# A graph layer: the first batch's source rows counted and multiplied instead of gathered

## The chip, the cores and the metric

The kernel runs on one core of a Trainium2 chip. A core has a matrix engine (PE, with its weight loads shown as PEld), a vector engine (DVE), an activation engine (ACT), GpSimd (POOL) and SyncE (SP, which only issues DMAs here). The metric is the device time of one execution in microseconds (us); the median of the runs is compared. Besides, one execution is recorded by the profiler; its span runs from its first to its last recorded instruction.

## What is computed

One attention layer on a graph of 12,500 nodes with 64 features and 400,000 edges with 64 features, which are sorted by destination. `W_attn` has 192 rows and one column, so an edge's raw score is a number for its source plus one for its destination plus one for its own features. The softmax runs over the edges that end in the same node.

```
h_src = x[src];  h_dst = x[dst]
e = leaky_relu(concat(h_src, h_dst, efeats) @ W_attn + b_attn, 0.01)
m = concat(h_src, efeats) @ W_ne
alpha = softmax of e over the edges of one dst
z = segment_sum(alpha * m, dst)
out = layernorm(x + relu(concat(x, z) @ W_out))
```

`src` is uniform over the nodes. `dst` is floor(12500 u^2) of a uniform u, sorted: the low nodes have many edges (node 0 alone has some 3,600, and the first 8,192 edges end in nodes 0 to 5) and the high ones few.

## The kernel before

**Groups, lots, batches.** The edges are cut into 782 groups of 512: 128 partitions by T = 4 edges in a row. Sixteen groups make a batch (47 of these, then 12, 12 and 6 groups: 50 batches), and SG = 4 groups make a lot, so that a batch has four lots. Since the edges are sorted, a group has its destinations in a narrow window of nodes, `widths[k]` wide (4 nodes in the first batches, 48 at most).

**Source rows.** `gather` (L199 to L210) fetches x[src] for a lot into one buffer `zx` by 16 indirect DMAs on POOL, each for 128 edges. There are ZB = 8 such buffers, two batches' worth, so that batch k's lot i is gathered into the buffer that batch k-2's lot i used, when the matmuls that read it (L428) are through. Rows come from `table` in DRAM: 65 numbers each, the node's score as a source ahead of its 64 features. The table must be built first (L518 to L523), so batch 0 is "plain": it is gathered from `x` itself while the table is built, and its source scores are computed from the rows (L244, L246).

**The front** (L448 to L539) reads x into `xall` (13 DMAs on SP), computes each node's score as a destination (`dots`, L489) and as a source, writes the table, broadcasts each group's first destination to all partitions (`d0b`, L529 and L530), and fetches each group's window of destination scores by seven indirect DMAs on POOL (`window`, L483). The first window stands behind three lots' gathers in POOL's order; batch 0's scores need it.

**A batch** has three stages, in an order written out by hand for PE, DVE, ACT and SP (the loop L705 to L786):
- `scores` (L231) for each lot: edge features (`ze`, loaded by SP at L192, three buffers) times their weights, the source's and the destination's score, sums into `yraw`. It also copies `ze` beside the gathered rows (L238), so that a row of `zx` holds both, and makes `hot`, one-hot over the window of destinations (L249).
- `softmax` (L329): running maxima and sums along the edges by scans, with edge values carried between partitions by small PE transposes (`to_line` L265, `to_col` L268). At four places, where DVE waits for PE, it calls `fill`, which is `meanwhile` (L690): one lot's finished products are added into `acc` (L445), and half a lot of waiting products is issued.
- `weights` (L408), one-hot times softmax, and `products` (L423): for each 128 edges a matmul with `zx` as the stationary side and the weights as the moving one. Stationary rows 1 to 128 are the source's and the edge's features, so a lot's sums for both come out of one matmul. The first NOW = 2 lots' products follow the softmax; the other two go into the fills of the next batch's softmax.

`add_in` adds a lot's PSUM bank into `acc`, a ring of 3072 nodes with 128 rows (source features above, edge features below). When a block of NBC = 4 x 128 nodes can get no more edges (`due`, computed ahead from the expected positions with a safety), `finish0` to `finish3` turn it into output rows, and its piece of the ring is cleared. The first block is due after batch 10.

**Safety.** Positions and widths are written into the code, so columns such as `fars`, `ups`, `lates` and `earlies` collect how far the data strays; `raised` (L557) makes one flag of them, and with the flag up a second kernel path computes the result in another way.

The changed places are the constants, `listed`, `edges`, `scores`, `products`, `add_in`, the front's order and the loop.

Of the kernel before, what the change touches and what calls it, by code (L numbers as in the profile page):

```python
# [9 lines left out]
F32 = mybir.dt.float32  # L10
I32 = mybir.dt.int32
# [19 lines left out]
EW = 65  # L31
ZB = 8
HB = 5
RING = 3072
NBC = 4
LATE = 8.0
NOW = 2

BF16 = mybir.dt.bfloat16
# [3 lines left out]
def sorted_path(ctx, tc, x, dst, idx, edge, w_ne, w_attn, b_attn, w_out, out, flag):  # L43
# [41 lines left out]
    widths = [width(b0 + G) for b0, G in zip(starts, sizes)]  # L85

    eps_col = const.tile([P, 1], F32, name="eps_col")
    nc.vector.memset(eps_col, EPS)
# [23 lines left out]
    d0i = const.tile([1, NG], I32, name="d0i")  # L112
    lates = const.tile([P, len(sizes)], F32, name="lates")
    d0b = const.tile([P, NG], F32, name="d0b")
    fars = const.tile([P, len(sizes)], F32, name="fars")
    ups = const.tile([P, len(sizes)], F32, name="ups")
    earlies = const.tile([P, len(sizes)], F32, name="earlies")
    both = const.tile([P, D], F32, name="both")
# [32 lines left out]
    pps = psum.tile([P, 512], F32, name="pps", bufs=1)  # L151
    pp, pens, w_dst = cut(pps, T * BS, 2 * P, D)
    pp = pp.rearrange("p (t g) -> p t g", t=T)
    pens = pens[0:1].rearrange("o (k i) -> o k i", k=2)

    def listed(k):

        g0, G = starts[k], sizes[k]
        srcs = chunks.tile([P, BS, 2 * T], I32, name="srcs", bufs=3)
        last = g0 + G == NG  # L160
        if last:
            nc.vector.memset(srcs, 0)
            nc.sync.dma_start(out=srcs[0:RP, G - 1], in_=idx[NG - 1, P - RP:P])
        for a in range(0, G - last, SG if k == 0 else G):
            b = min(a + (SG if k == 0 else G), G - last)
            nc.sync.dma_start(out=srcs[:, a:b], in_=idx[g0 + a:g0 + b].rearrange("g p c -> p g c"))
        return srcs
# [63 lines left out]
    def scores(g0, n, zx, drel, b0, plain):  # L231

        b = g0 - b0
        r = rows_of(g0, n)
        Sk = widths[starts.index(b0)]
        ze, wrow = fetched.pop(g0)
        nc.scalar.activation(win[0:r, 0:n, 0:Sk], wrow[0:r, 0:n, :], AF.Copy)  # L237
        nc.scalar.activation(zx[0:r, 0:n, :, EW:EW + D], ze[0:r, 0:n], AF.Copy)  # L238
        pr = feats.tile([P, SG, T, D], F32, name="pr", bufs=1)
        nc.vector.tensor_tensor(pr[0:r, 0:n], ze[0:r, 0:n],  # L240
                                w_edge[0:r].unsqueeze(1).to_broadcast([r, n, T, D]), op=OP.mult)
        nc.vector.tensor_reduce(ysum[0:r, 0:n], pr[0:r, 0:n], axis=AX.X, op=OP.add)  # L242
        if plain:
            nc.vector.tensor_tensor(pr[:, 0:n], zx[:, 0:n, :, 1:EW],  # L244
                                    w_src.unsqueeze(1).unsqueeze(1).to_broadcast([P, n, T, D]), op=OP.mult)
            nc.vector.tensor_reduce(zx[:, 0:n, :, 0], pr[:, 0:n], axis=AX.X, op=OP.add)  # L246
        nc.vector.tensor_tensor(ysum[0:r, 0:n], ysum[0:r, 0:n], zx[0:r, 0:n, :, 0], op=OP.add)
# [6 lines left out]
        nc.vector.tensor_tensor(at[0:r, 0:n], hot[0:r, 0:n],  # L254
                                win[0:r, 0:n, 0:Sk].unsqueeze(2).to_broadcast([r, n, T, Sk]), op=OP.mult)
        sdst = tiny.tile([P, SG, T], F32, name="sdst")
        nc.vector.tensor_reduce(sdst[0:r, 0:n], at[0:r, 0:n], axis=AX.X, op=OP.add)  # L257
        nc.vector.tensor_tensor(yraw[0:r, :, b:b + n].rearrange("p t g -> p g t"), ysum[0:r, 0:n], sdst[0:r, 0:n], op=OP.add)
        return hot

# [162 lines left out]
    def products(k, pg, zx, w, groups, r=P):  # L423

        for g in groups:
            for t in range(T):
                if k + 2 < len(sizes):
                    nc.tensor.matmul(pg[:, g, :], zx[:, g, t, 1:EW + D], w[:, g, t, :],  # L428
# [6 lines left out]
    def add_in(g0, n, pg, b0, fac):  # L435
# [4 lines left out]
        for g in range(n):  # L440
            if g == 0 and fac is not None:
                a1 = acc[:, ds(vs[0], 1)]
                nc.vector.tensor_scalar(a1, a1, fac, None, op0=OP.mult)
            ag = acc[:, ds(vs[g], Sk)]
            nc.vector.tensor_tensor(ag, ag, pg[:, g, :], op=OP.add)  # L445

# [8 lines left out]
    nc.scalar.dma_start(out=wout, in_=w_out.rearrange("(h k) o -> k h o", h=2))  # L455
    lists = {0: listed(0)}
    xts = []
# [12 lines left out]
    nc.sync.dma_start(out=d0i, in_=dst.rearrange("(o n) -> o n", o=1)[:, 0:E:GE])  # L470
    lists[1] = listed(1)
    sd = const.tile([P, NB], F32, name="sd")
# [8 lines left out]
    with before:  # L481
# [22 lines left out]
        with tc.manual_schedule(engines={EngineType.DVE, EngineType.Pool, EngineType.Activation, EngineType.PE, EngineType.SP}):  # L504
            lots0 = [(g0, min(SG, sizes[0] - g0)) for g0 in range(0, sizes[0], SG)]
            ahead = [gather(g0, n, lists[0], 0, True) for g0, n in lots0[:-1]]
            for c0 in range(0, NB, CB):
# [24 lines left out]
            for r in range(RING, N, RING):  # L532
                nc.vector.tensor_scalar(turns_, d0f, float(RING), -float(RING), op0=OP.is_ge, op1=OP.mult)
                nc.vector.tensor_tensor(d0i if r + RING >= N else d0f, turns_, d0f, op=OP.add)
            window(0)
            ahead += [gather(g0, n, lists[0], 0, True) for g0, n in lots0[-1:]]
            for k in range(1, NW):
# [8 lines left out]
    nc.tensor.transpose(pwt[0:D, 0, :], wne, ident)  # L546
    wt = work.tile([D, NBC, P], F32, name="xtt", bufs=3)
    nc.vector.tensor_copy(wt[:, 0, :], pwt[0:D, 0, :])
# [29 lines left out]
    def finish1(c0, pxt):  # L578
        n = min(NBC, NB - c0)
        xtt = work.tile([D, NBC, P], F32, name="xtt", bufs=3)  # L580
        nc.scalar.activation(xtt[:, 0:n, :], pxt[0:D, 0:n, :], AF.Copy)
        return c0, xtt
# [65 lines left out]
    for c0 in range(0, NB, NBC):  # L648
# [4 lines left out]
        due[k].append(c0)  # L653
    nc.vector.memset(earlies, 0.0)

    with loop:
# [33 lines left out]
        def meanwhile():  # L690

            add_up(1)
            some_products()

        with tc.manual_schedule(engines={EngineType.PE, EngineType.DVE, EngineType.Activation, EngineType.SP}):
            ready = {}
            for k in range(2):
                as_floats(k, lists[k])
                ready[k] = slots_of(k)
            about = between(0)  # L700
            at_ends(*about)
            nc.scalar.dma_start(out=wins[0], in_=wks[0])
            ahead_of(*flat[0])
            turned_x, ready_x, open_ = finish0(0), None, None
            for k, G in enumerate(sizes):  # L705
# [3 lines left out]
                more = k + 2 < len(sizes)  # L709
                if more:  # L710
# [3 lines left out]
                tiles = [ahead.pop(0) if ahead else gather(g0, n, srcs, b0, k == 0) for g0, n in lots[k]]  # L714
                parts = []
                after = None
                for i, (g0, n) in enumerate(lots[k]):
                    if g0 in follows:
                        ahead_of(*follows[g0])
                    if k == 0 and i == len(lots[k]) - 1:  # L720
# [3 lines left out]
                    hot = scores(g0, n, tiles[i], drel, b0, k == 0)  # L724
                    parts.append((g0, n, tiles[i], hot))
                    if i == 0:
# [14 lines left out]
                    if final and i == 1:  # L741
# [6 lines left out]
                        fronts.append(front(*x1, pps[:, T * BS + 2 * P + D:512].rearrange("p (j d) -> p j d", d=D), False))  # L748
                fac, carry = softmax(k, about, carry, meanwhile)
                while later:  # L750
                    some_products()
# [474 lines left out]
```

## Time and profile before

| what | value |
|---|---|
| median of 3 timed runs | 4614.47 us (4612.89 to 4615.68) |
| the profiled execution's own time | 4585.16 us |
| its span | 4583.4 us |
| granted TensorE clock, mean | 0.995 |
| first gather / first gather of batch 2 / of batch 3 | 4.87 / 194.81 / 286.26 us |
| first gather of batch 47 / last gather | 4341.90 / 4523.8 us |
| DMA traffic | 51 GB/s over the span |

Busy time of each engine in some stretches of the span, in us, with the number of instructions:

| stretch | PE | DVE | ACT | POOL |
|---|---|---|---|---|
| 0 to 97 | 6.14 (16) | 61.69 (106) | 12.06 (34) | 68.62 (78) |
| 97 to 177 | 13.00 (61) | 25.40 (60) | 9.64 (24) | 60.38 (64) |
| 195 to 287 | 29.86 (141) | 24.73 (70) | 10.33 (27) | 60.94 (65) |
| 470 to 562 | 29.70 (141) | 26.50 (75) | 10.56 (28) | 60.50 (65) |

In the profile's lines "L206" is line 206 of the kernel; "zx<-table,srcs" names what an instruction writes and reads; "x64" is a number of instructions. A line of a timeline gives start, duration, engine, line and operation, and in brackets the engine's idle time ahead of it with what ended it; "issue" is waiting that the profile can't name, "remote" a signal from outside the engine. Neighbouring instructions of one kind share a line. An fp32 matmul appears as two records of PE, each with its weight load.

### The profile page before, as it was taken

The numbers are of one execution on the slowest core, as the hardware profiler recorded it, in microseconds if no ns is written. First come the engines' busy times: TensorE is split into PE (matmuls) and PEld (weight loads), VectorE is DVE, ScalarE is ACT, GpSimd is POOL, SyncE is SP. The second block draws the span as 40 slices with busy tenths as digits, with TensorE's granted clock in tenths as the row PEclk, the third lists the DMA queues.
The fourth block names the chain that finished last, engine by engine and source line by source line (L and its number), as shares of the span: only waits on it lengthen the run. The fifth ranks groups of instructions, "written<-read, shape, count | busy, mean of one in ns | idle before, by whom it ended". The sixth has DMA issues, their size and how long they took to land. (4 is left out here: it accounts for less than half of the span.)

```text
span 4583.4 us, 29058 instructions
## 1 busy us (share of the span) xinstructions
PE 1591.8 (35%) x7451; PEld 1535.3 (33%) x7451; DVE 1682.0 (37%) x4079; ACT 629.6 (14%) x1550; POOL 2959.3 (65%) x3142
## 2 busy tenths in 40 slices
PE   0223323232333333333343343333333433343444
PEld 0223323232333333333343333333332433343344
DVE  6223323232333223423343343334333434343445
ACT  1101101011111111111111111111111112111212
POOL 7666666666666666666666666666666666666662
PEclk9999999999999999999999999999999999999998
DMA  8222222122222221222222221222222222222221
GB/s 115 47 44 47 59 44 48 43 59 45 44 55 54 46 45 44 66 45 45 45 67 46 46 56 42 52 54 56 46 59 46 47 46 59 57 46 48 51 46 34
DMA packets 453432, 234.18 MB, mean 51 GB/s; under 512 B 298849, under 2 KB 403272, under 8 KB 453256
## 3 DMA queue, kind: packets, MB, share of 16 engines
q0 software_dynamic: 100320, 104.34, 11.7%
q1 hardware_dynamic: 349892, 127.61, 11.5%
q8 instruction: 60, 0.98, 0.1%
q14 instruction: 116, 0.95, 0.1%
q10 hardware_dynamic: 3044, 0.29, 0.1%
HBM read 225.34 MB, written 6.66 MB: 51 GB/s over the span
## 5 line engine op out<-in xcount | busy, mean ns | idle before, releaser
L206 POOL DMA_INDIRECT zx<-table,srcs x3064 | 2890.7, 943 | 1537.1 <-issue 1301.2
L428 PEld LDWEIGHTS pg<-w,zx 128*128 128x128 f32 x6112 | 1359.4, 329 | 970.9 <-issue 829.8
L428 PE MATMUL pg<-w,zx 128*128 128x12 f32 (+11 forms) x6112 | 1335.8, 376 | 987.8 <-issue 842.0
L240 DVE TENSOR_TENSOR pr<-ze,fixed 128x1024 f32<-128x1024 f32 (+2 forms) x200 | 239.2, 1196 | 511.5 <-ACT fixed L237 325.5
L265 PE MATMUL lines<-ident,bnd 128*1 128x128 f32 x200 | 58.7, 396 | 849.8 <-issue 476.6
L265 PEld LDWEIGHTS lines<-ident,bnd 128*1 128x1 f32 x200 | 9.7, 85 | 861.8 <-issue 500.8
L382 DVE TENSOR_TENSOR_SCAN dens<-rw,lines 1x64 f32<-1x64 f32 (+2 forms) x50 | 13.6, 272 | 637.3 <-remote 517.8
L242 DVE TENSOR_REDUCE fixed<-pr 128x16 f32<-128x1024 f32 (+2 forms) x200 | 240.7, 1204 | 8.9 <-DVE pr L240 2.1
L387 DVE SCALAR_TENSOR_TENSOR soft<-mask,lines,soft 128x128 f32<-128x128 f32 x50 | 18.0, 360 | 597.4 <-remote 512.5
L268 PE MATMUL lines<-ident,line 1*128 1x1 f32 x200 | 36.9, 251 | 534.5 <-issue 279.2
L363 DVE SCALAR_TENSOR_TENSOR soft<-pen,lines,soft 128x128 f32<-128x128 f32 x50 | 18.0, 360 | 549.2 <-remote 457.1
L268 PEld LDWEIGHTS lines<-ident,line 1*128 1x128 f32 x200 | 28.4, 199 | 547.1 <-issue 281.9
L238 ACT ACTIVATE zx<-ze 128x1024 f32<-128x1024 f32 (+2 forms) x200 | 207.9, 1039 | 10.7 <-issue 1.8
L445 DVE TENSOR_TENSOR acc<-acc,pg 128x12 f32 (+11 forms) x782 | 141.0, 180 | 181.7 <-remote 108.6
L268 PE MATMUL lines<-ident,keep 1*128 1x1 f32 x49 | 12.8, 261 | 488.3 <-issue 176.7
L268 PEld LDWEIGHTS lines<-ident,keep 1*128 1x128 f32 x49 | 8.7, 177 | 499.2 <-issue 353.6
L237 ACT ACTIVATE fixed<-wrow 128x144 f32<-128x144 f32 (+10 forms) x200 | 50.6, 253 | 712.4 <-issue 355.5
L257 DVE TENSOR_REDUCE sdst<-pr 128x16 f32<-128x192 f32 (+12 forms) x200 | 116.8, 584 | 27.0 <-DVE pr L254 12.3
L249 DVE TENSOR_TENSOR hot<-fixed,drel 128x576 bf16<-128x576 f32 (+10 forms) x200 | 117.9, 589 | 17.2 <-issue 5.9
L254 DVE TENSOR_TENSOR pr<-hot,fixed 128x576 f32<-128x576 bf16 (+10 forms) x200 | 116.9, 585 | 18.2 <-issue 5.4
L272 ACT ACTIVATE line<-dens 1x256 f32<-1x256 f32 x50 | 32.7, 653 | 657.5 <-DVE dens L384 484.7
L403 ACT ACTIVATE keep<-part,dens 1x1 f32<-1x1 f32 x49 | 14.4, 293 | 708.5 <-DVE part L401 528.1
(153 smaller groups left out, 1497.7 us busy)
## 6 DMA issues: line engine op xcount, KB each, us to landing
ze<-in_edge_dram SPq DMA_DIRECT2D x188, 512.0 KB
zx<-table,srcs POOLq DMA_INDIRECT x3064
table<-xall SPq DMA_DIRECT2D x7, 455.0 KB
out_dram<-yo SPq DMA_DIRECT2D x24, 128.0 KB
ze<-in_edge_dram SPq DMA_DIRECT2D x8, 384.0 KB
edges_of<-in_dst_dram SPq DMA_DIRECT2D x187, 8.1 KB
srcs<-in_idx_dram SPq DMA_DIRECT2D x46, 64.0 KB
xall<-in_x_dram SPq DMA_DIRECT2D x13, 224.0 KB
```

What stands on the lines that cost most here:

```text
L206: nc.gpsimd.indirect_dma_start(out=zx[0:r, g, t, 1:EW] if plain else zx[0:r, g, t, 0:EW], out_offset=None, in_=x[:, :] if plain else table ...
L237: nc.scalar.activation(win[0:r, 0:n, 0:Sk], wrow[0:r, 0:n, :], AF.Copy)
L238: nc.scalar.activation(zx[0:r, 0:n, :, EW:EW + D], ze[0:r, 0:n], AF.Copy)
L240: nc.vector.tensor_tensor(pr[0:r, 0:n], ze[0:r, 0:n], w_edge[0:r].unsqueeze(1).to_broadcast([r, n, T, D]), op=OP.mult)
L242: nc.vector.tensor_reduce(ysum[0:r, 0:n], pr[0:r, 0:n], axis=AX.X, op=OP.add)
L249: nc.vector.tensor_tensor(hot[0:r, 0:n], slots[0:r, 0:Sk].unsqueeze(1).unsqueeze(1).to_broadcast([r, n, T, Sk]), drel[0:r, :, b:b + n].rea ...
L254: nc.vector.tensor_tensor(at[0:r, 0:n], hot[0:r, 0:n], win[0:r, 0:n, 0:Sk].unsqueeze(2).to_broadcast([r, n, T, Sk]), op=OP.mult)
L257: nc.vector.tensor_reduce(sdst[0:r, 0:n], at[0:r, 0:n], axis=AX.X, op=OP.add)
L265: nc.tensor.transpose(in_order(line), col, ident)
L268: nc.tensor.transpose(col, line, ident[0:1, 0:1])
L428: nc.tensor.matmul(pg[:, g, :], zx[:, g, t, 1:EW + D], w[:, g, t, :], start=(t == 0), stop=(t == T - 1))
L445: nc.vector.tensor_tensor(ag, ag, pg[:, g, :], op=OP.add)
```

## The change

Batch 0 (DB = 1 batch, DG = 16 groups, 8192 edges) is no longer gathered. Batch 1 takes its place as the plain one, gathered from `x`: two lots ahead of the first window, two behind it. What batch 0 needs of its sources is had in two other ways.

*Scores* (`looked_up`): the source's number is split into a low part (its 7 low bits) and a high part (its block of 128 nodes). For each group a matmul with a one-hot column (`pick`) spreads the 512 low parts over all partitions; ACT makes of them a one-hot in fp32 (square of the difference to the partition's number, then relu of one minus that); four fp32 matmuls with it multiply the 128 x 98 table of source scores that lies in SBUF (`s_src`), and DVE picks the right block with a mask, and sums.

*Features*: batch 0's products take only the edge features (`ze` as the stationary side, rows 64 to 127 of the sums), all four lots right after the softmax. The source features come later: in batch 2 to batch 9 two groups each (EACH = 2, at the third and fourth lot) go through `dense_part`. For each group, four one-hots over (block of the source, one of NOD = 5 destination places) made by ACT, four over the low part times the softmax share (`kept`) made by DVE, and four fp32 matmuls of 490 columns sum these into a matrix of shares by source and destination; `dense_sum` adds it, in the fills of the softmax, into `counts` (128 x 98 x 9). In batch 10 `resolve` multiplies `counts` with x by 13 fp32 matmuls of 512 columns, sums the parts that belong together, and adds the result into the top rows of `acc` for nodes 0 to 8. `kept` is corrected after batch 1's softmax for the destination that both batches share.

Besides: `ze` has four buffers in place of three, `xtt` two in place of three; batch 0's and 1's index lists and a second copy of batch 0's (`raw`) are loaded in another order; output blocks due before batch 10 would wait for it; two columns of the safety flag are new, which check the places written into the code (`bases`).

```diff
+DB = 1
+NOD = 5
+EACH = 2
...
-        ze = feats.tile([P, SG, T, D], F32, name="ze", bufs=3)
+        ze = feats.tile([P, SG, T, D], F32, name="ze", bufs=4)
...
-        nc.scalar.activation(zx[0:r, 0:n, :, EW:EW + D], ze[0:r, 0:n], AF.Copy)
+        dense = g0 < DG
+        if dense:
+            steps = looked_up(g0, n)
+            next(steps)
+        else:
+            nc.scalar.activation(zx[0:r, 0:n, :, EW:EW + D], ze[0:r, 0:n], AF.Copy)
...
+    def looked_up(g0, n):
+        sources = tiny.tile([P, SG, T], F32, name="sources")
+        founds = []
+        for g in range(n):
+            wide = psum.tile([P, SG, P], F32, name="pg", bufs=4).rearrange("p a b -> p (a b)")
+            nc.tensor.matmul(wide, pick[:, g0 + g:g0 + g + 1].to_broadcast([DG, P]), low_row.rearrange("g p t -> g (p t)"),
+                             start=True, stop=True)
+            nc.scalar.activation(wide, wide, AF.Square, bias=p_col)
+            hot = work.tile([P, P, T], F32, name="big", bufs=4)
+            nc.scalar.activation(hot.rearrange("l p t -> l (p t)"), wide, AF.Relu, scale=-1.0, bias=1.0)
+            found = psum.tile([P, SG, P], F32, name="pg", bufs=4)[:, :, 0:NB]
+            for t in range(T):
+                nc.tensor.matmul(found[:, t, :], hot[:, :, t], s_src, start=True, stop=True)
+            founds.append(found)
+            if g == 0:
+                yield
+            hits = work.tile([P, T, NB], BF16, name="hits", bufs=2)
+            nc.vector.tensor_tensor(hits, count_[:, 0:NB].unsqueeze(1).to_broadcast([P, T, NB]),
+                                    high[:, :, g0 + g:g0 + g + 1].to_broadcast([P, T, NB]), op=OP.is_equal)
+            nc.vector.tensor_tensor(found, found, hits, op=OP.mult)
+            nc.vector.tensor_reduce(sources[:, g], found, axis=AX.X, op=OP.add)
+        yield sources
+
+    def dense_part(g):
+        lows = work.tile([P, T, P], F32, name="lows", bufs=2)
+        highs = []
+        for t in range(T):
+            hi = work.tile([P, P, T], F32, name="big", bufs=4).rearrange("l p t -> l (p t)")[:, 0:PLACES]
+            nc.scalar.activation(hi, places, AF.Square, bias=place[:, t, g:g + 1])
+            nc.scalar.activation(hi, hi, AF.Relu, scale=-1.0, bias=1.0)
+            nc.vector.tensor_scalar(lows[:, t, :], count_, low[:, t, g:g + 1], kept[:, t, g:g + 1],
+                                    op0=OP.is_equal, op1=OP.mult)
+            highs.append(hi)
+        to = psum.tile([P, SG, P], F32, name="pg", bufs=4).rearrange("p a b -> p (a b)")[:, 0:PLACES]
+        for t in range(T):
+            nc.tensor.matmul(to, lows[:, t, :], highs[t], start=(t == 0), stop=(t == T - 1))
+        return g, to
+
+    def dense_sum(g, to):
+        at = counts[:, :, bases[g]:bases[g] + NOD]
+        nc.vector.tensor_tensor(at, at, to.rearrange("p (h n) -> p h n", n=NOD), op=OP.add)
+
+    def resolve():
+        both_ways = psum.tile([P, SG, P], F32, name="pg", bufs=4).rearrange("p a b -> p (a b)")
+        for h0 in range(0, NB, HC):
+            m = min(HC, NB - h0)
+            nc.tensor.matmul(both_ways[0:m * ND, 0:m * D], counts[:, h0:h0 + m, :].rearrange("l h n -> l (h n)"),
+                             xall[:, h0:h0 + m, 1:EW], start=(h0 == 0), stop=(h0 + m == NB), skip_group_check=True)
...
-                if k + 2 < len(sizes):
+                if k < DB:
+                    nc.tensor.matmul(pg[D:P, g, :], zx[:, g, t, :], w[:, g, t, :],
+                                     start=(t == 0), stop=(t == T - 1))
+                elif k + 2 < len(sizes):
...
-            ahead = [gather(g0, n, lists[0], 0, True) for g0, n in lots0[:-1]]
+            first = [(g0, SG) for g0 in range(DG, starts[DB + 1], SG)]
+            ahead = [gather(g0, n, lists[DB], DG, True) for g0, n in first[:2]]
...
             window(0)
-            ahead += [gather(g0, n, lists[0], 0, True) for g0, n in lots0[-1:]]
+            ahead += [gather(g0, n, lists[DB], DG, True) for g0, n in first[2:]]
...
         def meanwhile():
+            if counted:
+                dense_sum(*counted.pop(0))
             add_up(1)
             some_products()
...
+                    if k > DB and waits_ and i >= len(lots[k]) - EACH:
+                        counted.append(dense_part(waits_.pop(0)))
+                    elif k > DB and not waits_ and k == solved and i == 2:
+                        resolve()
...
-                    if i < NOW:
+                    if i < NOW or k < DB:
```

More of the change, by code (lines that the diff above doesn't have):

```diff
@@ L85, in sorted_path, with node_at @@
     widths = [width(b0 + G) for b0, G in zip(starts, sizes)]
+    DG = starts[DB]
+    def node_at(e, sigmas):
+        e = e + sigmas * (e * (1.0 - e / E)) ** 0.5
+        return int(N * (max(e, 0.0) / E) ** 2)
+    bases = [node_at(g * GE, -5.0) for g in range(DG)]
+    assert all(node_at((g + 1) * GE, 5.0) < b + NOD for g, b in enumerate(bases))
+    ND = bases[-1] + NOD
+    HC = min(8, P // ND)
+    assert NB * NOD == PLACES and ND <= NBC * P
     eps_col = const.tile([P, 1], F32, name="eps_col")
@@ L470, in sorted_path @@
     nc.sync.dma_start(out=d0i, in_=dst.rearrange("(o n) -> o n", o=1)[:, 0:E:GE])
-    lists[1] = listed(1)
+    for k in range(DB):
+        lists[k] = listed(k)
+    raw = pre.tile([DG, P, 2 * T], I32, name="raw", bufs=1)
+    nc.sync.dma_start(out=raw, in_=idx[0:DG])
     sd = const.tile([P, NB], F32, name="sd")
@@ L546, in sorted_path @@
     nc.tensor.transpose(pwt[0:D, 0, :], wne, ident)
-    wt = work.tile([D, NBC, P], F32, name="xtt", bufs=3)
+    wt = work.tile([D, NBC, P], F32, name="xtt", bufs=2)
     nc.vector.tensor_copy(wt[:, 0, :], pwt[0:D, 0, :])
@@ L579, in finish1 @@
         n = min(NBC, NB - c0)
-        xtt = work.tile([D, NBC, P], F32, name="xtt", bufs=3)
+        xtt = work.tile([D, NBC, P], F32, name="xtt", bufs=2)
         nc.scalar.activation(xtt[:, 0:n, :], pxt[0:D, 0:n, :], AF.Copy)
@@ L654, in sorted_path @@
     nc.vector.memset(earlies, 0.0)
+    solved = DB + 1 + (DG + EACH - 1) // EACH
+    moved = [c0 for k in range(solved + 1) for c0 in due[k]]
+    due[0:solved + 1] = [[] for _ in range(solved)] + [moved]
     with loop:
@@ L703, in sorted_path @@
             ahead_of(*flat[0])
[L704 removed]
+            turned_x, ready_x, open_ = None, None, None
+            waits_, counted = list(range(DG)), []
             for k, G in enumerate(sizes):
@@ L709, in sorted_path @@
                 more = k + 2 < len(sizes)
-                if more:
+                if more and k + 2 != DB:
                     lists[k + 2] = listed(k + 2)
@@ L713, in sorted_path @@
                     neighbours(k + 1)
-                tiles = [ahead.pop(0) if ahead else gather(g0, n, srcs, b0, k == 0) for g0, n in lots[k]]
+                tiles = [None if k < DB else ahead.pop(0) if ahead else gather(g0, n, srcs, b0, False) for g0, n in lots[k]]
                 parts = []
@@ L719, in sorted_path @@
                         ahead_of(*follows[g0])
-                    if k == 0 and i == len(lots[k]) - 1:
+                    if k == DB and i == 1:
                         for j in range(1, NW):
```

94 lines of the change are left out of this document (81 added, 13 removed).

## The prediction

> **What bounds the kernel now.** I read the page first: the busy shares (part 1) and the costliest groups (part 5).
>
> ```profile
> PE 1591.8 (35%) x7451; PEld 1535.3 (33%) x7451; DVE 1682.0 (37%) x4079; ACT 629.6 (14%) x1550; POOL 2959.3 (65%) x3142
> ...
> L206 POOL DMA_INDIRECT zx<-table,srcs x3064 | 2890.7, 943 | 1537.1 <-issue 1301.2
> ```
>
> POOL leads with 65%, nearly all of it in the gathers of L206: 0.94 us each, and the 0.30 us between two of them makes a step of 1.248. 3128 gathers and 7 windows by 1.248 are 3912 us of a span of 4583.4. The rest is waiting, and the timeline of POOL shows where (start, duration, then in brackets the idle time ahead):
>
> ```profile
> 175.85 0.94 POOL L206 DMA_INDIRECT zx<-table,srcs  x1 [0.30 <-issue]
> 194.81 0.94 POOL L206 DMA_INDIRECT zx<-table,srcs  x1 [18.01 <-ACT bnd L354]
> ...
> 263.00 0.94 POOL L206 DMA_INDIRECT zx<-table,srcs  x1 [8.57 <-issue]
> 286.26 0.94 POOL L206 DMA_INDIRECT zx<-table,srcs  x1 [3.59 <-issue]
> ```
>
> The eight buffers hold two batches, so 128 gathers run through to 176.8. At 194.81 batch 2 begins, when batch 0's first products have freed a buffer. Batch 3 begins at 286.26, batch 6 at 561.88, batch 47 at 4341.90: 41 batches of 92.2. Of these 64 x 1.248 = 79.9 are gathers and 12.3 are stops at the start of a tile. The stops hardly depend on the work: 8.57 + 3.59 in one batch, 6.1 + 6.1 in another, their length going with how long POOL ran before (3.6 after 20 us, 6.3 after 40, 8.6 after 60). Period and stops stay the same when a batch also writes an output block (12 fp32 transposes and matmuls as 20 records, 7 DVE and 5 ACT instructions): 91.6 to 92.4 with one and without from batch 10 to 37, 93 to 94 in six of the ten periods after it. So a gather costs 92.2 / 64 = 1.44 us in the steady part, and other engines' work is nearly free there.
>
> Last I read PE and DVE in the first 300 us.
>
> ```profile
> 138.69 8.91 PE L428 MATMUL pg<-w,zx 128*128 128x4 f32 x41 [7.53 <-remote]
> ...
> 151.96 0.17 PE L428 MATMUL pg<-w,zx 128*128 128x4 f32 x1 [2.63 <-issue]
> 154.76 0.17 PE L428 MATMUL pg<-w,zx 128*128 128x4 f32 x1 [2.64 <-issue]
> ...
> 199.30 3.58 PE L428 MATMUL pg<-w,zx 128*128 128x4 f32 x16
> ```
>
> ```profile
> 86.06 1.22 DVE L244 TENSOR_TENSOR pr<-zx,lines 128x1024 f32<-128x1024 f32 x1
> ...
> 107.17 0.22 DVE L254 TENSOR_TENSOR pr<-hot,fixed 128x64 f32<-128x64 bf16 x1 [1.17 <-issue]
> 108.57 0.22 DVE L257 TENSOR_REDUCE sdst<-pr 128x16 f32<-128x64 f32 x1 [1.18 <-DVE pr L254]
> ```
>
> Some 8 to 16 us after POOL has gone over to rows of `table` all engines turn slow: 41 records of L428 still go at 0.21 us, then one every 2.1 to 2.8; DVE instructions of 0.22 start 1.4 apart. This lasts from 104 to some 15 us after POOL stopped (192). Batch 0's softmax takes 24 us in it (110.7 to 134.8), against 13.5 outside. I call this the slow stretch. In the plain phase before (rows of x, to 97) DVE runs at full pace.
>
> **The change part by part.** Its sum goes: after = X + (4583.4 - 286.26) + dense parts + resolve, where X is the start of batch 3's first gather, and 4297.1 from there to the end stays, if POOL is fed as now.
>
> *Removed:* batch 0's 64 gathers. At 1.44 that is 92 us if POOL never waits for the new work; 80 at 1.248. Batch 1's gathers take their place (plain), batch 2's follow at 97. So the 128th still ends at 176.8, but with one batch more behind it: what frees batch 3's buffer is batch 1's first lot of products, and these need all of batch 0's lookups, softmax and products first. So the gain is what X comes to lie below 286.26.
>
> *Start of the lookups.* The window of L485 moves from 48 gathers to 32, some 20 us earlier. Scores begin 8.6 us behind it now (68.51, 77.09), so about 55 after; but the front grows: 2 iotas on POOL (0.16 each at L100, inside its 3.40 wait), a memset of 128x882 (0.75 by L543's 2.66 for 3120), two reduces, some 9 DVE and 5 ACT instructions of 0.2 to 0.3, and two loads more on SP ahead of the windows' addresses. I take 64.
>
> *One lookup*, a group: a bf16 product over 512 columns (no such row; between 0.17 for 4 columns and 0.88 for 384 fp32 columns, L529; 0.4 taken), two ACT passes of 128x512 (0.57, L581, on half the partitions), four fp32 products of 98 columns, 8 records between 0.21 (L428) and 0.42 (L575, 128 columns; 0.3 taken, 2.4 in all), three hops of 0.2: 4.3 us, because PE and ACT work in turn. DVE's three passes over 128x392 (0.55 each by L493) lie beside the next group. A lot: 17 + 2 = 19. Two lots fit from 64 to 102. L238 and L244/246 (1.05, 2.5) go, which is in the 2.
>
> *In the slow stretch* (104 to 192): PE's 41 free records are 4.5 groups, at the softmax's stretch of 24/13.5 about 8 us each, 36 us; then 9 records at 2.6 make 23 us a group, 2.3 in the 52 left. 6.8 of the 8 groups are done by 192, the rest by 199. From there all runs at full pace, since POOL stands still: softmax 13.5 (213), the first lot's 32 records at 0.2135 (220). Batch 1's first edge load may start only now, as the fourth `ze` buffer covers one lot and batch 0 holds four; SP stands behind it with all that follows on its queue (later `ze`, rows, neighbours; 12 us until DVE has it, with the row of `wins`: 232). Then four lots of batch 1's scores with L244 and L246, 6.2 each as at 77.1 to 83.3 (257), softmax 13.5 (270), 32 records (277). **X = 277**, 9 below. From both sides: no slow stretch gives 64 + 76 = 140 for the lookups and X = 218; nothing done from 104 to 192 gives 8 x 4.3 + 15 after it, and X = 303.
>
> *Dense parts*, two in each of batches 2 to 9: 16 ACT passes of 128x490 (0.55: 9 us), 8 DVE passes of 128x128 (0.36 each by L363), two sums of 128x490 (0.6), and 8 fp32 products of 490 columns, 16 records at up to 1.1 (L529's 0.88 by 490/384), 12 to 18 us. PE has 62 us idle in such a batch (29.9 busy of 92), ACT 82. They stand ahead of the softmax's transposes; the second part's ACT waits for the first's products to free `big`, and behind it stand the softmax's ACT copies. Covered, they cost what an output block costs, 0 to 2; uncovered up to 13 (the ACT and PE time that then lies ahead of the softmax). The block's row is nearest, but ACT has three times its count: 2.5 taken, **+20** (0 to 104).
>
> *Resolve*, once at batch 10: 26 fp32 records of 512 columns at up to 1.2 (L529), 18 to 30 us PE, a multiply and a reduce over 128x512 (0.65 each), one small product. Hidden 0, uncovered 30; **+5** for the same reason. The masks for `kept` (four DVE passes of 128x64, 0.22) lie in X's 13.5 + 2; output block 0 moves by nothing (it was due at batch 10).
>
> Sum: 4583.4 - 9 + 20 + 5 = 4599 in span. The profiled execution took 4585.16, the runs' median 4614.47, so 31 us lie between span and median. **4630 us**, +0.3%.
>
> **Rivals.**
> 1. *The gain comes through* (chance 0.22). The slow stretch could belong to the recording alone: many small records at an even 0.7 us. Then lookups end at 140, X = 218 at most, and dense parts cost nothing: -68 to -75, 4543. Against it: the profiled run is no slower than the timed ones, though without slow stretches the stops would shrink and 3135 x 1.248 would end near 4000. [...]
> 2. *Half of it* (0.13): lookups slip through the slow stretch (X 250), dense parts at 0.5: -36 + 4 + 2, 4585.
> 3. *Nothing to tell* (0.14): X 270, dense parts at 1, or X 285 with dense parts free: within 9 us of 4614. 0.2%, or 9 us, is about what a measurement of this kernel can tell from no change.
> 4. *Dense parts move the softmax past a slow stretch* (0.16): it starts right as POOL resumes (286.26) and has 17 us of full pace; 10 us more of ACT and PE push its third step behind it, where such a step waited 27.5 us for a signal:
>
> ```profile
> 235.01 0.36 DVE L387 SCALAR_TENSOR_TENSOR soft<-mask,lines,soft 128x128 f32<-128x128 f32 x1 [27.48 <-remote]
> ```
>
>    Then tile 2 or 3 waits for its products in eight batches, 6 to 9 us each, +60; with X at 285 and resolve at 15, 4690. It decides once a batch's stops sum to over 14 instead of 12.3. Against it: stops keep their sum whichever tile they fall on.
> 5. *The fallback is taken* (under 0.01): a group's destinations would have to leave their five places; the range written into the code is far wider than the data's spread. It would show at once as a second path.
>
> **How the numbers follow.** Forecast 0.35 (its own range 4600 to 4670: X from 260 to 300, dense parts 1 to 5), rivals as given. Below 4605 lie rivals 1 and 2 and a little of the forecast's lower end: faster 0.36. Within 9 us: rival 3, 0.14. Slower: most of the forecast and rival 4, 0.50. The range takes in most of rival 1 and rival 4: 4540 to 4690.
>
> **What would show it.** X in POOL's timeline: 277 says the slow stretch was placed right; 218 and full-pace lookups beyond 104 say rival 1. The sum of POOL's stops in batches 4 to 11: 12 + 2.5 by my forecast, 12.3 if hidden, over 18 by rival 4. One lookup takes 4.3 us before 104. I am wrong from the start if POOL's steady period after batch 12 differs from 92.2, since 4297 us of the sum rest on it.

## The result and the profile after

The changed kernel takes 4656.53 us (median of 6 runs, 4654.52 to 4658.27), the kernel before 4612.72 on the same chip: a ratio of 1.0094, 95% interval 1.0081 to 1.0107, 44 us slower. A second series on another chip gave 4630.73 against 4584.46, 1.0102 (1.0085 to 1.0119). The forecast was 4630, within 4540 to 4690: the side was right, the size a third of what came.

The page of the changed kernel shows POOL still in the lead, with 64 gathers fewer:

```profile
PE 1697.6 (36%) x7751; PEld 1575.9 (34%) x7751; DVE 1742.9 (37%) x4232; ACT 727.1 (16%) x1713; POOL 2907.0 (62%) x3080
...
L244 POOL DMA_INDIRECT zx<-table,srcs x3000 | 2837.7, 946 | 1658.8 <-issue 1290.8
```

POOL is busy 52 us less and idle longer by more than that: the wait ahead of L244 has grown from 1537 to 1659. Its timeline has the place:

```profile
317.13 0.95 POOL L244 DMA_INDIRECT zx<-table,srcs  x1 [136.67 <-PE pg L557]
369.32 0.95 POOL L244 DMA_INDIRECT zx<-table,srcs  x1 [12.46 <-issue]
415.62 0.94 POOL L244 DMA_INDIRECT zx<-table,srcs  x1 [6.58 <-issue]
```

After its 128th gather POOL stands still for 137 us. Batch 3 begins at 317.13; before, it began at 286.26. Batch 3 then takes 98.5 us (a stop of 12.46 in its middle), the next ones 92.7 to 92.9.

PE's timeline shows what the gap is made of. L332 spreads the low parts of one group, L339 is its four products (8 records); one row of ACT is put between them, the first pass over what L332 made (L334):

```profile
82.83 2.19 PE L339 MATMUL pg<-s_src,big 128*128 128x98 f32 x8 [13.41 <-issue]
84.95 0.60 PE L332 MATMUL pg<-low_row,pick 16*128 16x512 bf16 x1
86.93 2.18 PE L339 MATMUL pg<-s_src,big 128*128 128x98 f32 x8 [1.38 <-issue]
89.05 0.60 PE L332 MATMUL pg<-low_row,pick 16*128 16x512 bf16 x1
...
105.65 0.66 ACT L334 ACTIVATE pg<-pg,p_col 128x512 f32<-128x512 f32 x1 [18.78 <-issue]
107.00 2.18 PE L339 MATMUL pg<-s_src,big 128*128 128x98 f32 x8 [17.35 <-ACT pg L334]
...
132.19 2.19 PE L339 MATMUL pg<-s_src,big 128*128 128x98 f32 x8 [22.48 <-ACT pg L334]
...
195.90 2.19 PE L339 MATMUL pg<-s_src,big 128*128 128x98 f32 x8 [10.58 <-ACT big L336]
...
200.00 2.18 PE L339 MATMUL pg<-s_src,big 128*128 128x98 f32 x8 [1.38 <-ACT big L336]
...
238.30 2.18 PE L339 MATMUL pg<-s_src,big 128*128 128x98 f32 x8 [1.38 <-ACT big L336]
```

Two groups go at 4.1 us, then one every 25.2 (107.00, 132.19, 157.40, 182.59), and from 196 on, 15 us after POOL's last gather, again one every 4.1. The last lookup ends at 240.5, and 76.6 us later batch 3 begins. The records themselves do not stretch: L332 has passed at 89.65 and eight records of L339 take 2.2 us as before. The wait lies between them: ACT's pass over what L332 made starts 16 us after L332's record.

### The profile page after: what moved, and what is told of

It is laid out like the page before. It is cut to its first block, busy times and chain, and to the rows that moved or that the text cites. A ratio compares the mean times of both kernels' runs of the same rounds, so it can differ in the third digit from the quotient of the medians.

```text
span 4656.6 us, 29877 instructions
## 1 busy us (share of the span) xinstructions
PE 1697.6 (36%) x7751; PEld 1575.9 (34%) x7751; DVE 1742.9 (37%) x4232; ACT 727.1 (16%) x1713; POOL 2907.0 (62%) x3080
## 3 DMA queue, kind: packets, MB, share of 16 engines
q0 software_dynamic: 98272, 102.21, 13.8%
## 4 chain that ended last, share of the span: by engine, by line
another core or an unknown queue 15%; issue 14%; DVE 10%; PE 5%; POOL 5%; ACT 2%; DMA 1%; DVEq 0%; ACTq 0%; POOLq 0%
POOL zx L244 5%; PE pg L557 4%; DVE pr L283 1%; DVE acc L575 1%; DVE hot L292 1%; DVE pr L297 1%; DVE sdst L300 1%; DVE fixed L285 1%; DMA zx<-table,srcs 1%; DVE w L540 1%; DVE level L516 0%; PE lines L391 0%; DVEq L566 0%; PE pg L754 0%
## 5 line engine op out<-in xcount | busy, mean ns | idle before, releaser
L244 POOL DMA_INDIRECT zx<-table,srcs x3000 | 2837.7, 946 | 1658.8 <-issue 1290.8
L557 PE MATMUL pg<-w,zx 128*128 128x12 f32 (+10 forms) x5984 | 1293.4, 373 | 1051.0 <-issue 957.2
L557 PEld LDWEIGHTS pg<-w,zx 128*128 128x128 f32 x5984 | 1317.5, 326 | 1036.8 <-issue 927.9
L394 PE MATMUL lines<-ident,line 1*128 1x1 f32 x200 | 36.7, 250 | 375.7 <-ACT line L398 292.9
L508 DVE TENSOR_TENSOR_SCAN dens<-rw,lines 1x64 f32<-1x64 f32 (+2 forms) x50 | 13.6, 272 | 426.1 <-remote 362.4
L394 PEld LDWEIGHTS lines<-ident,line 1*128 1x128 f32 x200 | 28.2, 197 | 387.2 <-ACT line L398 299.2
L494 ACT ACTIVATE soft<-turned 128x128 f32<-128x128 f32 x50 | 14.1, 281 | 851.6 <-DVE turned L493 695.8
L540 DVE TENSOR_TENSOR w<-hot,fixed 128x576 f32<-128x576 bf16 (+10 forms) x200 | 103.1, 577 | 0.2 <-ACT kept L910 0.2
L754 PE MATMUL pg<-both,acc 128*128 128x64 f32 x184 | 63.2, 447 | 54.9 <-DVE acc L575 53.9
```

What stands on the lines that cost most here:

```text
L244: nc.gpsimd.indirect_dma_start(out=zx[0:r, g, t, 1:EW] if plain else zx[0:r, g, t, 0:EW], out_offset=None, in_=x[:, :] if plain else table ...
L394: nc.tensor.transpose(col, line, ident[0:1, 0:1])
L540: nc.vector.tensor_tensor(w[0:r, 0:n], hot[0:r, 0:n], alpha[0:r, :, b:b + n].rearrange("p t g -> p g t").unsqueeze(3).to_broadcast([r, n, ...
```

## Experiments

Chips differ by about 1% here (the kernel before: 4584 to 4630, and 3982 on one chip that comes further down), so ratios and differences are taken against the kernel before on the same chip.

**The kernel before again** (no edit).

> The kernel before, unchanged, with its trace taken again. The changed kernel's trace shows a granted clock of 0.54 from 317 us on and a steady batch of 92.6 us; before's trace had 0.995 and 91.9. If the clock goes with the chip and not with the change, this trace shows a low clock, batches of some 92.5 and a span near 4611; then 31 us between before's profiled 4585 and its median 4613 are the clock's, and the steady part is no cost of the change. If the low clock is the change's own doing (its wide fp32 matmuls), this trace shows 0.99 again and a span near 4583.

Measured: 4630.2 against 4630.29, ratio 1.000; granted clock 0.995, batch 3 at 288.69, steady batches of 92.5. Here the profiled run and the median agree, so the 31 us between before's profiled run and its median are most likely one chip against another, and the low clock is the change's own. The next three runs, on the same chip, show that it costs nothing: from batch 11's first gather to batch 47's, e_none takes 3356.4 us at the full clock and e_nolook 3356.3 at the low one.

**Three kernels that leave out the new work**, to price each part.

```diff
 e_none, e_nolook
-            steps = looked_up(g0, n)
-            next(steps)
...
-        nc.vector.tensor_tensor(ysum..., next(steps)[:, 0:n] if dense else zx[0:r, 0:n, :, 0], op=OP.add)
+        if not dense:
+            nc.vector.tensor_tensor(ysum..., zx[0:r, 0:n, :, 0], op=OP.add)
 e_none, e_nodense
-            waits_, counted = list(range(DG)), []
+            waits_, counted = [], []
...
-                    elif k > DB and not waits_ and k == solved and i == 2:
+                    elif False:
```

> The changed kernel without lookups, dense parts and resolve: batch 0's source scores and source features are left out. It is the floor of the change. If the start is what costs (batch 3's first gather at 317 instead of 286), that gather starts near 205 to 215 (softmax and batch 1's scores partly in the slow stretch) and the time is some 4535 to 4550. If dense parts and resolve cost most of the 44 us, it is lower still, by 30 more: 4510.

> The changed kernel without lookups alone (batch 0's source scores are left out), dense parts and resolve kept. If the start costs and the dense parts are nearly hidden: within 15 us of the run without either, 4545 to 4565. If dense parts cost 5 us a batch: 4580 or more.

> The changed kernel with lookups but without dense parts and resolve (batch 0's source features are left out). If the start costs: 4640 to 4650, with batch 3's first gather still at 317. If dense parts and resolve are most of the 44 us: near 4615.

| kernel | us | ratio (95%) | batch 3 begins | batch 3 lasts | clock |
|---|---|---|---|---|---|
| before | 4630.3 | 1 | 288.69 | 92.46 | 0.995 |
| neither (e_none) | 4594.2 | 0.9928 (0.9911 to 0.9945) | 252.25 | 93.16 | 0.995 |
| dense parts only (e_nolook) | 4607.8 | 0.9955 (0.9938 to 0.9971) | 252.63 | 99.08 | 0.538 |
| lookups only (e_nodense) | 4657.0 | 1.0059 (1.0042 to 1.0076) | 317.55 | 93.17 | 0.995 |

The parts nearly add up: -36 for the 64 gathers, +63 for the lookups (batch 3's start moves by 65), +14 for dense parts and resolve; together +40 (before rounding), where the whole change showed +44 and +46 on other chips. Two things follow. The lookups are the loss. And even with no new work at all the 64 gathers bring 36 us, not the 92 of a batch: I had expected 4535 to 4550. The run without either shows why, in the timelines of batch 0's products (L554; PEld is the weight load), of the load of batch 1's first edge rows (L230, on SP's queue) and of the first scores of batch 1 (L282):

```profile
134.60 3.89 PE L554 MATMUL pg<-w,ze 128*64 128x4 f32 x35 [7.37 <-issue]
...
140.17 0.18 PEld L554 LDWEIGHTS pg<-w,ze 128*64 128x64 f32 x1 [1.66 <-issue]
141.57 0.17 PE L554 MATMUL pg<-w,ze 128*64 128x4 f32 x1 [2.62 <-issue]
142.97 0.18 PEld L554 LDWEIGHTS pg<-w,ze 128*64 128x64 f32 x1 [2.62 <-issue]
144.37 0.17 PE L554 MATMUL pg<-w,ze 128*64 128x4 f32 x1 [2.63 <-issue]
...
194.76 4.00 PE L554 MATMUL pg<-w,ze 128*64 128x4 f32 x37 [0.54 <-issue]
```

```profile
194.80 0.38 SPq L230 DMA_DIRECT2D ze<-in_edge_dram  x1
...
200.12 1.22 DVE L282 TENSOR_TENSOR pr<-ze,fixed 128x1024 f32<-128x1024 f32 x1 [59.09 <-ACT fixed L275]
```

35 matmuls go at full pace, then a pair of weight load and matmul mostly each 2.80 us, load and matmul 1.40 apart, until 195. The edge rows of batch 1 wait for the first lot of these products to give up its buffer, so batch 1's scores, which the kernel before runs while POOL gathers (147 to 188), start only at 200. POOL has long run out of buffers by then. What is late is the signal, more than the work: the first lot is 32 matmuls, which by the rows had started by 138, yet the load that waits for them goes off 57 us later, when the stretch ends. In the changed kernel, where POOL stands still by then, that load follows the first product by 3.6 us (255.95 and 259.53).

**POOL kept still during the lookups** (v_late).

The ordinary load of that list is left out as well; the new one is:

```diff
+                    if k == 0 and i == 3:
+                        lists[2] = chunks.tile([P, BS, 2 * T], I32, name="srcs", bufs=3)
+                        nc.scalar.dma_start(out=lists[2], in_=idx[starts[2]:starts[2] + BS].rearrange("g p c -> p g c"))
+                        as_floats(2, lists[2])
```

> The changed kernel, but batch 2's index list is loaded only behind batch 0's last lookup (by ACT), so that POOL gathers nothing from the table while the lookups run. If POOL's table gathers make the slow stretch: all 16 lookups at about 4.2 us, done near 160 instead of 241, batch 2's gathers from 163 to 243, batch 1's scores slowed from about 175 on, batch 3's first gather between 260 and 290, time 25 to 55 us below the changed kernel's 4657. If the lookups are slow by themselves (PE and ACT working in turn): they keep their 25 us a group, POOL only starts later, and the time is longer than 4657 by up to 60.

Measured: ratio 1.0082 (1.0065 to 1.0099). Soon after POOL stops at 100 the lookups of this run go at full pace, 4.1 us a group:

```profile
105.42 2.19 PE L339 MATMUL pg<-s_src,big 128*128 128x98 f32 x8 [15.73 <-ACT big L336]
...
109.52 2.18 PE L339 MATMUL pg<-s_src,big 128*128 128x98 f32 x8 [1.38 <-ACT big L336]
...
119.70 2.18 PE L339 MATMUL pg<-s_src,big 128*128 128x98 f32 x8 [1.38 <-ACT big L336]
```

The last ends at 168, and that much is as the first theory has it: POOL's gathering slows the lookups (25.2 us a group in the changed kernel, 4.1 here), they are not slow by themselves. But batch 3 begins at 313.63, far from the 260 to 290 expected: POOL resumes at 169.19, and batch 0's products, from 184 on, now lie in the slow stretch: 36 matmuls at full pace, then one pair per 2.1 to 3.5 us. The load of batch 1's first edge rows goes off at 256.19, 69 us after the first lot's last matmul started. The stretch had been moved from one part of batch 0's chain to the next.

**An earlier start** (v_early): ACT writes the window back and fetches batch 0's row ahead of `places_of`; `between(0)` and the second half of the work on places go behind the first lot.

> The changed kernel with the first window's rows written back and batch 0's row of it fetched ahead of the work on neighbours and places on ACT, so that the first lookup starts near 55 to 58 instead of 81.5. If what counts is how many groups are through before the slow stretch: 4 to 6 groups more are done by 104, batch 3's first gather near 280 to 290 and 27 to 37 us less than the changed kernel. If the slow stretch simply begins earlier with the work: no more than 10 us less.

Measured: 1.0091 (1.0074 to 1.0108), batch 3 at 317.00. The write-back moved from 68.55 to 57.36, the first ACT pass of a lookup only from 81.50 to 75.69, and the eighth group's spreading matmul is at 198.0 in both. So the first lookup came 6 us earlier, not 24, and the stretch set in 6 us earlier too (at 84 instead of 90), again after two groups: it began earlier with the work, as the second theory has it, and what gets through before 196 did not change. What four to six groups more would bring, this run does not show; part of the work that was moved back (L394) now lies in the stretch itself.

**Overlap, or fewer records.** In the slow stretch a lookup could be one late signal of fixed length, or PE could give up its records at a fixed pace. v_pipe issues the next group's L332 and its two ACT passes ahead of a group's products; v_bf16 halves the records of the products:

```diff
-    s_src = const.tile([P, NB], F32, name="s_src")
+    s_src = const.tile([P, NB], BF16, name="s_src")
...
-            hot = work.tile([P, P, T], F32, name="big", bufs=4)
+            hot = work.tile([P, 2 * P, T], BF16, name="big", bufs=4)[:, 0:P, :]
```

> The changed kernel with the next group's spreading matmul and its two ACT passes issued ahead of a group's four fp32 matmuls, so that a late signal between PE and ACT is waited for once for two groups. If the 25.2 us of a slow group are one late signal: some 13 us a group, the lookups end near 195, batch 3's first gather some 40 earlier. If they are PE's pace (9 matmuls and 9 weight loads, 18 records of 1.4 us): still 25 us a group in the slow stretch, and at most 10 us less in all, from the groups at full pace (4.1 to about 3.3).

> The changed kernel with the lookups' one-hots and the 98 columns of source scores in bf16 (batch 0's source scores are rounded to bf16), so that each of the four matmuls of a group is one record of PE instead of two: 5 matmuls and 5 weight loads a group, 10 records for 18. If PE gives up one record each 1.4 us while POOL gathers: 14.0 us a slow group instead of 25.2, some 3 groups more by 192, batch 3's first gather near 295 to 300 and some 20 us less. If a slow group is one late signal of fixed length: still 25 a group in the stretch, and only the groups at full pace gain (4.1 to about 3.0), 11 us.

Measured: v_pipe 1.0066 (1.0049 to 1.0083), batch 3 at 302.89. The spreading matmuls now come in pairs, but three groups take 75.6 us in the stretch (109.90 to 185.50), 25.2 each as before; its 14 us come from groups at full pace, 4 from a third one ahead of the stretch and 10 from quicker ones behind it, a little more than I gave the second theory. v_bf16: 1.0023 (1.0013 to 1.0032), batch 3 at 285.42, ten groups done by 192 where the changed kernel had six, and in its PE timeline:

```profile
113.69 0.52 PE L339 MATMUL pg<-s_src,big 128*128 128x98 bf16 x4 [12.94 <-ACT pg L334]
...
127.70 0.52 PE L339 MATMUL pg<-s_src,big 128*128 128x98 bf16 x4 [12.96 <-ACT pg L334]
...
141.69 0.52 PE L339 MATMUL pg<-s_src,big 128*128 128x98 bf16 x4 [12.94 <-ACT pg L334]
```

14.0 us a group, as 10 records of 1.40 would have it; 18 records of 1.40 are the 25.2, and a pair is the 2.80 of the products above. So in the slow stretch PE's work moves on by one record, weight load or matmul, per 1.40 us, however short the record is. In the products' rows the records themselves stand that far apart; in the lookups' rows they stand close together, and it is the signal behind them that comes later by 1.40 us for each of them. A late signal it is, then, but not one of fixed length. The pace is not the same everywhere: in v_late and in the kernel before, pairs also come at 2.1 us.

**Plain gathers for batch 2 as well** (m_plain2): the fourth argument of its `gather` and `scores` made true.

> The changed kernel with batch 2 too gathered plain, from x, its source scores computed from the rows as batch 1's. If it is the table's rows (65 numbers, written shortly before) that slow the engines: the lookups run at about 4.2 us to the end, done near 160, and batch 3's first gather is at 240 or below. If any run of gathers does it: 25 us a group as before, the gather at 317 and up to 10 more for L287 and L289 in batch 2.

Measured: 1.0086 (1.0069 to 1.0103), the spreading matmuls at 110.4, 135.6, 160.8, 186.0, batch 3 at 316.88. Rows of x slow the lookups just as rows of the table do, 25.2 us a group with either. The prediction had tied the stretch to the table; in the changed kernel too it set in at 90, while POOL still gathered rows of x (to 93).

**POOL kept still until batch 0's first products**, alone (v_l2) and with two more edits (v_pl2d: the overlap of v_pipe, and dense parts in batches 4 to 11).

```diff
-                if more and k + 2 != DB:
+                if more and k + 2 != DB and k:
                     lists[k + 2] = listed(k + 2)
...
+                if k == 0:
+                    lists[2] = listed(2)
+                    as_floats(2, lists[2])
                 if more:
                     ready[k + 2] = slots_of(k + 2)
```

> The changed kernel with three edits: the next group's spreading matmul ahead of a group's four products; batch 2's index list loaded only behind batch 1's first edge load, so that POOL gathers nothing from 100 us until batch 0's first products are through; dense parts in batches 4 to 11 instead of 2 to 9. If the slow stretch on batch 0's chain is what costs: lookups done near 150, POOL resumes near 175, batch 1's scores and softmax partly in the slow stretch, batch 3's first gather near 260, and the period after it 93 instead of 98.5: some 50 us below the changed kernel and 5 to 25 below the kernel before. If what the lookups lose comes back as POOL's idle time: batch 3's first gather at 300 or later and no gain on before.

> The changed kernel with one edit: batch 2's index list is loaded behind batch 1's first edge load, so that POOL stands still from 100 us until batch 0's first products are through. In the run where it only waited for the last lookup, the lookups ended at 168 instead of 241, but batch 0's 128 product records then fell into the slow stretch and batch 3's first gather came at 313.6. If that is the whole story: lookups again to 168, products in 14 us at full pace, POOL from some 193, batch 1's scores and softmax partly slow, batch 3's first gather near 285, and some 30 us less than the changed kernel (1.002 to 1.004 of before). If the gain of the run with three edits came from the other two: 310 or more, and no more than 5 us less.

Measured: v_pl2d 4597.66 against 4609.1, ratio 0.9977 (0.9968 to 0.9986): 0.2% faster than the kernel before, and within the first theory's 5 to 25 us below it. POOL's timeline:

```profile
175.07 0.94 POOL L244 DMA_INDIRECT zx<-table,srcs  x1 [76.09 <-issue]
269.25 0.94 POOL L244 DMA_INDIRECT zx<-table,srcs  x1 [14.44 <-issue]
315.52 0.95 POOL L244 DMA_INDIRECT zx<-table,srcs  x1 [6.54 <-issue]
```

Batch 3 begins at 269 instead of 317 and lasts 92.9 instead of 98.5; lookups and products run at full pace in the pause of 76 us (the last lookup ends at 149.15; products from 164.68, 96 matmuls in 10.4 us, the load of the next edge rows at 168.26). The three edits were not run apart on such a chip: the overlap alone (v_pipe) brought batch 3 to 302.89, the moved dense parts come after its start, so the step from 302.89 to 269.25 is put down to the pause by difference.

v_l2 met another condition, in which its expectation can't be judged: on that chip the kernel before took 3981.97 us, v_l2 3975.0 (0.9984, 0.9974 to 0.9994). Its POOL timeline has no stop at the start of batch 3 (251.79), and of its waits only one is long, the pause before batch 2 (sum, number, longest):

```profile
250.54 0.95 POOL L244 DMA_INDIRECT zx<-table,srcs  x1 [0.30 <-issue]
251.79 0.94 POOL L244 DMA_INDIRECT zx<-table,srcs  x1 [0.30 <-issue]
```

```profile
POOL zx L244 <- issue: 960.3, 2909, 74.2
```

Every batch takes 79.95 us there, 64 times 1.249. Lookups take 4.1 us from the first on: the first six while POOL still gathers (to 97.6), the others in the pause. Later work beside POOL's gathers goes at full pace as well: 64 matmuls of batch 1's products take 13.8 us from 215.80, where the kernel before did 59 at full pace and then one pair each 2.8 us. No slow stretch is seen.

**The changed kernel again**, to see it in that condition.

> The changed kernel itself, unchanged, once more. The run before this one met a condition in which the kernel before took 3982 us instead of 4609, with batches of 79.95 us and no stops of POOL and no slow stretch in the changed one's trace. If that condition holds here too: lookups 4.1 us each from about 71 on, done near 144, batch 3's first gather near 215 to 225 with POOL never short of a buffer for long after it, 3940 to 3955 us, so 0.7 to 1 per cent faster than before: the change's sign then hangs on the slow stretch alone. If the other condition holds (before at 4605 to 4635): 25.2 us a slow lookup, the gather at 317, a ratio near 1.009 as in the first result.

Measured: the usual condition, batch 3 at 316.30, 1.0102. How the change does where no stretch exists was not measured.

## Why the prediction was right in direction and short in size

*The bound and the steady part* held. Batches 4 to 11 took 91.8 to 93.1 us on average, so stops of 12 to 13, in every run of the usual condition, with and without dense parts, and rival 5 (the fallback) did not occur.

*The direction* came out right for another reason than the one given, and that is luck. The working had the start gain 9 us and the dense parts with resolve lose 25; the start lost 31 and the dense parts with resolve lost 12. The total came as near as 27 us because the two misses, 40 and 13, have opposite signs.

*X was the step that failed*: 277 forecast, 317 measured, +31 against before instead of -9. It lies past the upper of the two bounds (303) too, which took eight groups as done before the stretch. It failed in the lookups, not behind them: from their end to batch 3 I had 78 us, and it took 76.6. Three terms were off. The first lookup's products came at 83, not soon after 64: the window's rows were fetched early, but ACT, which writes them back, stood behind DVE's small instructions for the places (11.13 us ahead of L435), and between these DVE sat idle for up to 4.8 us by then. The stretch set in at 90 instead of 104, after two groups rather than eight. And the 41 "free" records at 8 us a group did not come; the pace was 25.2 (I had 23) from the third group on. That makes 6 groups done by 192 instead of nearly 15, and the last at 240.5 instead of 199. One lookup at full pace was near, 4.3 forecast and 4.1 measured, but its terms as listed (0.4, two of 0.57, 2.4, three hops of 0.2) sum to 4.5, and the hops had no row behind them: the changed kernel shows 0.03 to 0.05 between the steps, 0.60 for the spreading, 0.66 and 0.60 on ACT and 2.2 for the products.

*What the gathers are worth.* The prediction named 92 us as the gain if POOL never waited and let X decide. The run with neither lookups nor dense parts puts X at 252 and the gain at 36. Its reason stood in my own working, the edge load behind batch 0's products, but I had these products, and the signal of their end, at full pace; where lookups are quick they fall into the stretch.

*Dense parts*: +20 forecast, 12 measured between the two runs that differ in them: 5.9 in batch 3 and 5.9 over the eight batches after it, resolve (+5 forecast) included in the latter. 1.8 of the 13.6 between their medians I can't place. The place was right and so was the mechanism of rival 4 for one batch: in batch 2 the second part's matmuls come at 334 to 353, a pair of products in 5.6 us, the softmax's first transpose follows at 353, and tile 2 of batch 3 waits 12.46. It does not repeat; later, POOL's stops keep their sum, as argued.

*Span to median*: the 31 us I added are most likely a difference between chips, as the kernel before taken again has it.

*Rival 1* stood on the slow stretch vanishing. In the usual condition it is there in every run. In one condition, on one chip, it vanished with POOL's stops, and the kernel before took 3982 us, close to the 4000 worked out there and some 630 less than the 4609 of another chip; that all of this is the stretch is argued from the stops (12 us in each of some 50 batches), not shown. But the trace of that run is recorded like the others, so recording alone does not make it; and as every run here carries a span and a clock, none is free of recording. What the runs show is the pace, mostly 1.40 us for each record whatever it does, after a first run at full pace (35 matmuls in e_none), with signals late by 57 us there, all while POOL gathers. What holds the signals back was not shown, nor whether POOL's issuing or the traffic of its gathers sets the pace.

## What to carry to other kernels

Taking work off the bounding engine brings only what its next input allows (here 36 us of the 92 that a batch takes): look first at how far ahead that engine may run, and price the chain that frees its buffers. Price new work at the pace of the stretch in which it will lie, and count instructions as well as their durations; here 18 short records cost 25 us. When a step starts late, look at when the signal came that it waited for, and not only at when the work ahead of it passed (57 us apart in e_none). Where a busy engine slows the others, pausing it on purpose can pay if the pause covers the whole critical chain: up to the last lookup it gained next to nothing (v_late), up to the first products it went with a gain over the kernel before (v_pl2d).

## What the runs showed of the hardware that was not expected

- While POOL issues gathers back to back, PE's work moves on by one record (weight load or matmul) per 1.40 us, in places per 1.05, after a first run at full pace (35 matmuls in e_none, 41 and 59 in the kernel before). The signals of PE's ends come late with it, by 57 us in e_none and 69 in v_late. Full pace is back 5 us (v_late) to 15 us (the changed kernel) after POOL's last gather. Both rows of x and rows of the table do it. One chip of those met, on which the kernel before took 3982 us, did not show it: lookups took 4.1 us beside POOL's gathers (v_l2).
- The granted TensorE clock had means of 0.54 to 0.56 in every kernel with dense parts, and 0.995 in those without. In the changed kernel it fell with the first of them, which starts at 324.56: 1.00 to 330 us, 0.50 to 0.55 from 340 on. It cost nothing that could be seen: sixteen matmuls of the products take 3.4 to 3.6 us at either clock, and the 36 batches from the 11th on take the same time (3356 us).
